# A chain of long convolutions and a Haar layer: tiles kept as sums and differences of neighbouring columns, and the columns of 48 channels by VectorE

## The chip, the cores and the metric

The kernel runs on one core of a Trainium2 chip. The metric is the device time in microseconds (us) of one execution. The core's engines are TensorE (PE; its weight loads are listed as PEld), VectorE (DVE), ScalarE (ACT), GpSimd (POOL) and SyncE (SP), which here only issues DMAs.

## What is computed

The input x has 4 images of 64 channels of 256 x 256 float32. It goes through four layers, and every layer's output is the next one's input.

Layers 0, 1 and 3 are long convolutions. Each channel has two causal filters of length 256, one along the height and one along the width, which a small network with sines makes from a table of positions. In short:

```python
k = einsum('ijk,imk->ijmk', hx, hy)[0]            # a separable filter per channel
y = irfft2(rfft2(x) * rfft2(k) / fft_size)[..., :256, :256]
out = y + x * bias[:, None, None]
```

Layer 2 is a two-dimensional Haar transform, a mixing of the channels with soft thresholds, and the inverse transform:

```python
f1 = haar2d(x)
for i in range(2):
    f4 = einsum('bchw,oc->bohw', f1 * v[i], conv_w[i])
    acc = acc + sign(f4) * relu(abs(f4) - tau[i])
out = haar2d(acc, inverse=True) + x
```

The first level of the Haar transform along the width takes the sum and the difference of each pair of neighbouring columns; its inverse does the same in the last place.

## The kernel before, in words

**Convolutions.** A channel of an image is one tile of 128 x 2 x 256 (256 KB). Because the filter is separable, a layer is two products with triangular Toeplitz matrices. `first` (L264) multiplies along the height and hands the result over transposed ("a", copied from PSUM by ACT, L275), `second` (L279) multiplies along the width, and DVE adds the input times the bias (`residual`, L292). Each product (`contract`, L258) is four matmuls, two of 256 columns (L261) and two of 128 (L262). A float32 matmul stands twice in the records. The Toeplitz tile t comes by DMA from a padded filter in DRAM (`toeplitz`, L249, out of `pads`): row p of it is the filter shifted by p, and both axes' filters lie in one tile. The networks that make the filters (`filters`, L169) run at the start.

**Haar forward and mixing.** For layers 0 and 1 of an image, `convolutions` (L322) runs over 64 channels. After layer 1, `pairs` (L335) takes the sums and the differences of neighbouring columns on DVE (L337, L338), from a tile y1 with one buffer of its own. Both go to DRAM (`keep`), and the sums through further levels: the two longest on DVE, five on POOL (L350, L351). ACT and DVE split the tile into two fp32r parts (L369, L374), PE transforms along the height (L381), and the coefficients go to DRAM. `mixing` (L402) then takes 64 groups of rows: a matmul over channels (L449), scaling and thresholds on ACT and DVE (L468 to L488), and the results are added into one large tile z (L494), which holds one image in four chunks of 16 channels.

**Inverse.** `inverse` (L517) goes over the 64 channels. The transform along the height is done in one of two ways. For chunks 1 to 3 (48 channels) DVE does it in place in z, level by level (`level`, L302, `halve`, L297, two operations each, L299 and L300). For chunk 0 (the first 16 channels) PE does it: after the rows' matmuls (L541, L542) ACT and DVE split the result into two parts (`halves`, L548, L549), and two matmuls of 512 columns apply the matrix `hb` (`cols`, L555). ACT copies a channel out of z (L534), and PE transforms along the width. Then `join` (L560) adds the kept half-transformed tile r (L563) and undoes the first level: sum and difference into the even and odd columns (L566, L567). Layer 3 follows at once (`last`, L607), and ACT's queue stores its output. In images 0 to 2 every third channel (`put_off`, 21 of 64) is stored in `late` instead, and its layer 3 runs beside image 3's mixing (`convolution`, L614).

**What sets the order.** Every step is put into a list with a time in ticks, which is its channel's or group's tick plus an offset out of `PLACE` (L26). The list is sorted and traced in that order, and the compiler's scheduler orders each engine's instructions by it as far as their data are ready, so work without a wait can move forward. Every engine then executes in the fixed order that results. Image b+1's convolutions lie beside image b's mixing. DMAs of x, filters, `keep`, coefficients and r are all issued by SP's queue, in order, each once its buffer is free. Buffers: "in" 3 (inputs), "res" 1 (y1, and t of `join`), "y" 5, "co" 3; filters 6.

## Time and profile before

| | us |
|---|---|
| runs shown | 2872.78, 2874.51, 2877.79; median 2874.51 |
| the profiled execution | 2874.07, of which span 2872.3 |
| granted TensorE clock in it | 0.999 |
| PE, DVE, ACT, POOL busy | 2827.1, 2494.9, 2080.3, 334.4 |
| HBM | 426.77 MB read, 219.48 MB written |

A line of the profile's groups gives line, engine, operation, output and inputs, shape and count; then busy time in us, mean length of one in ns, and the engine's idle time just before, with what ended it. A line of the timeline gives start, length, engine and operation. A line of busy times by stage gives the stage in us from the start, its length, each engine's busy time with the number of instructions, the granted clock, and the share and rate of the DMA engines. Matmuls overlap in the records, so the distance between starts tells more of them than their lengths.

### The profile page before, as it was taken

The page shows a single profiled execution, that of the slowest core. Times are in us where ns is not written, and L with a number is a line of the kernel's source. Part 1 is how long each engine was busy: PE and PEld are TensorE (multiplying, and loading weights), DVE is VectorE, ACT ScalarE, POOL GpSimd, SP SyncE. Part 2 cuts the span into 40 slices and gives each one's busy share as a digit, 9 for nine tenths or more (in the row PEclk, how much of TensorE's full clock was granted, in tenths as well). Part 3 has the DMA queues.
Part 4 walks back from the last instruction along what each step waited for, and adds up shares of the span by engine and source line. Part 5 has one row for each costly group of instructions (what it writes and reads, how often), then busy time and mean ns, then how long its engine had stood idle before and what let it go on. Part 6 is the DMA issues. An engine that isn't in the chain of part 4 may idle for free. (4 is left out here: it accounts for less than half of the span.)

```text
span 2872.3 us, 52434 instructions
## 1 busy us (share of the span) xinstructions
PE 2827.1 (98%) x16592; PEld 2555.6 (89%) x16592; DVE 2494.9 (87%) x4255; ACT 2080.3 (72%) x4950; POOL 334.4 (12%) x644
## 2 busy tenths in 40 slices
PE   9999999999999999999999999999999999999999
PEld 7899998898888898998898998998898998888998
DVE  4655558999999779999999779999999779999985
ACT  2333338999995558998985658999995659998554
POOL 0111111121121001221221001121121000000000
PEclk9999999999999999999999999999999999999999
DMA  6878787776667986777777986777777988787786
GB/s 182 249 231 230 232 232 227 207 208 204 205 209 213 289 254 198 214 213 214 209 207 236 299 255 196 213 214 216 208 208 235 297 266 235 229 238 212 224 241 201
DMA packets 599367, 649.77 MB, mean 226 GB/s; under 512 B 48465, under 2 KB 517044, under 8 KB 598964
## 3 DMA queue, kind: packets, MB, share of 16 engines
q1 hardware_dynamic: 536996, 578.61, 68.9%
q10 hardware_dynamic: 62096, 67.82, 6.7%
q8 instruction: 134, 2.20, 0.3%
q14 instruction: 141, 1.16, 0.1%
HBM read 426.77 MB, written 219.48 MB: 225 GB/s over the span
## 5 line engine op out<-in xcount | busy, mean ns | idle before, releaser
L261 PE MATMUL py<-t,a 128*128 128x256 f32 x3072 | 922.5, 382 | 9.5 <-ACT a L275 8.7
L275 ACT COPY a<-pa 128x512 f32<-128x512 f32 x768 | 478.8, 623 | 498.6 <-PE pa L262 455.2
L473 ACT ACTIVATE f<-px,vt 128x64 f32<-128x64 f32 x2816 | 610.5, 367 | 101.6 <-DVE f L468 101.1
L262 PEld LDWEIGHTS py<-t,a 128*128 128x128 f32 x3072 | 583.4, 190 | 79.3
L262 PE MATMUL py<-t,a 128*128 128x128 f32 x3072 | 590.0, 274 | 0.0
L261 PEld LDWEIGHTS py<-t,a 128*128 128x128 f32 x3072 | 497.3, 191 | 51.2 <-ACT a L275 19.0
L449 PE MATMUL px<-wb,f 128*128 128x256 f32 x2048 | 487.6, 380 | 7.6 <-ACT f L473 7.6
L449 PEld LDWEIGHTS px<-wb,f 128*128 128x128 f32 x2048 | 369.0, 190 | 50.0 <-ACT f L473 10.5
L351 POOL TENSOR_TENSOR sd<-less 128x128 f32<-128x128 f32 (+4 forms) x320 | 190.8, 596 | 1858.7 <-DVE less L350 1519.9
L534 ACT COPY zc<-z 128x512 f32<-128x512 f32 x256 | 282.1, 1105 | 108.1 <-PE pw L542 99.0
L484 DVE TENSOR_TENSOR mag<-mag,vt 128x1024 f32<-128x1024 f32 x256 | 316.6, 1237 | 12.3 <-ACT mag L477 11.5
L488 DVE SCALAR_TENSOR_TENSOR mag<-mag,f 128x1024 f32<-128x1024 f32 x256 | 316.6, 1238 | 0.0
L261 PE MATMUL pa<-t,y 128*128 128x256 f32 x1024 | 309.1, 384 | 6.8 <-DVE y L292 5.2
L261 PE MATMUL pa<-t,x 128*128 128x256 f32 x1024 | 305.9, 381 | 0.5 <-DMA t<-pad 0.5
L477 ACT ACTIVATE mag<-f 128x1024 f32<-128x1024 f32 x256 | 295.7, 1155 | 2.8 <-DVE z L494 0.4
L374 DVE TENSOR_TENSOR sp<-sd,sp 128x512 fp32r<-128x512 f32 x256 | 179.8, 702 | 129.3 <-ACT sp L369 128.2
L480 ACT ACTIVATE f<-f 128x1024 f32<-128x1024 f32 x256 | 285.8, 1116 | 3.5
L261 PE MATMUL pa<-t,u 128*128 128x256 f32 x772 | 233.2, 384 | 6.5 <-ACT w L548 2.8
L292 DVE SCALAR_TENSOR_TENSOR y<-x,bsb,py 128x512 f32<-128x512 f32 x256 | 190.9, 746 | 41.9 <-PE py L262 41.0
L262 PEld LDWEIGHTS pa<-t,x 128*128 128x128 f32 x1024 | 194.6, 190 | 26.3
L262 PEld LDWEIGHTS pa<-t,y 128*128 128x128 f32 x1024 | 194.5, 190 | 26.3
L292 DVE SCALAR_TENSOR_TENSOR y<-y,bsb,py 128x512 f32<-128x512 f32 x256 | 190.7, 745 | 26.0 <-PE py L262 25.6
(73 smaller groups left out, 4412.3 us busy)
## 6 DMA issues: line engine op xcount, KB each, us to landing
t<-pad SPq DMA_DIRECT2D x768, 256.0 KB, 4.1
x<-in_x SPq DMA_DIRECT2D x256, 256.0 KB, 3.7
coef<-co SPq DMA_DIRECT2D x256, 256.0 KB, 3.2
f<-coef SPq DMA_DIRECT2D x256, 256.0 KB, 3.2
r<-keep SPq DMA_DIRECT2D x256, 256.0 KB, 4.1
out_y<-y ACTq DMA_DIRECT2D x193, 256.0 KB, 4.3
keep<-sums SPq DMA_DIRECT2D x256, 128.0 KB, 2.8
keep<-sd SPq DMA_DIRECT2D x256, 128.0 KB, 2.8
```

Of the source, the lines that this page charges most:

```text
L261: nc.tensor.matmul(ps[:, m, :], src[:, 0, m * P : (m + 1) * P], t[:, ::-1], start=True, stop=False)
L262: nc.tensor.matmul(ps[:, m, P:], src[:, 1, m * P : (m + 1) * P], t[:, : P - 1 : -1], start=False, stop=True)
L275: nc.scalar.copy(a, s["p" + new])
L292: nc.vector.scalar_tensor_tensor(y, s[res], bsb[:, layer, c : c + 1], s["p" + new], ALU.mult, ALU.add)
L351: engine.tensor_tensor(t[:, :, :, half:length], v[..., 0], v[..., 1], ALU.subtract)
L449: nc.tensor.matmul(ps[:, q, h, :], f[:, q, h * P : (h + 1) * P], wb.rearrange("p r n -> p (r n)"), start=True, stop=True,)
L473: nc.scalar.mul(f4[:, j], px[:, j], scale(g, 0)[:, j : j + 1])
L477: nc.scalar.activation(mag, st[g]["f4"], AF.Abs)
L480: nc.scalar.activation(st[g]["f4"], st[g]["f4"], AF.Sign)
L484: nc.vector.tensor_sub(mag, mag, over(g, 1, 16))
L488: nc.vector.scalar_tensor_tensor(mag, mag, 0.0, st[g]["f4"], ALU.max, ALU.mult)
L534: nc.scalar.copy(a.rearrange("p h k i -> p (h k) i"), z[:, c // 16, :, :, c % 16].rearrange("p i x -> p x i"))
```

## The change

*Representation.* On load, each input tile is replaced by its sums (even columns) and differences (odd columns) of neighbours, made by POOL (`butterflies`, `pairs` now at 0.1; the load moves from 0.714 to -1.0). Layers 0 and 1 run on such tiles. The filter along the width is changed to match: its Toeplitz matrix in the new basis, with the halves for going back, is made from sums and differences of the filter at three shifts, in seven small DVE operations per layer. `pads` gets two rows per axis, and a Toeplitz tile is read in steps of two rows, by one transfer with three levels of addresses (two transfers for the first two channels of layer 0). y1 then holds sums and differences already: two residuals of 128x256 write them to `sums` and `sd`, and the DVE steps L337 and L338 are gone. In the inverse `join` writes u in the new basis, in two operations of 128x256, without t, L566 and L567. After layer 3 POOL forms the output's columns (`neighbours`; for the very last channel DVE), and the store moves from 4.537 to 5.2. The put-off channels keep the old form: for them `join` does what it did, and a fourth filter, `pads[3]`, is unchanged in its values.

*Columns.* In images 0 to 2 chunk 0 is treated as chunks 1 to 3 are: levels on DVE, without `halves` and `cols`. All four chunks' levels get new places beside the mixing, and those placed at or after the inverse's start may not be scheduled ahead of the last `join` before them (`stay`). In image 3 `halves`, `cols` and the places stay.

*Buffers.* "in", "res" and "y" become one set of nine, in which also the new tiles and late inputs lie.

```diff
 ROW = S + P
+EARLY = 2
 ...
 GT = 4
-BUFS = {"res": 1, "y": 5, "co": 3}
+BUFS = {"y": 9, "co": 3}
 ...
 PLACE = {
-    "load": 0.714,
+    "load": -1.0,
+    "pairs": 0.1,
+    "bands": 0.714,
     "a0": 1.643,
 ...
     "y1 sum": 4.429,
-    "pairs": 4.639,
     "keep": 4.929,
 ...
     "y3 sum": 3.542,
-    "out": 4.537,
+    "neighbours": 3.543,
+    "out": 5.2,
     "level": 0.6,
 ...
     "l y3 sum": 2.783,
-    "l out": 4.4,
+    "l out": 4.8,
     "l mix load": -0.977,
 ...
     scales = dram.tile([S // 4 // GT, P, 2, GT, 16], F32, name="scales")
-    pads = [dram.tile([C, 2, ROW], F32, name=f"pad{layer}") for layer in range(3)]
+    pads = [dram.tile([C, 2, 2, ROW], F32, name=f"pad{layer}") for layer in range(4)]
     late = dram.tile([B, C, P, 2, S], F32, name="late")
 ...
             done["out"] = nc.vector.scalar_tensor_tensor(f[:, :S], ps, dsb[:, S:], dsb[:, :S], ALU.mult, ALU.mult)
-            for axis, queue in enumerate((nc.scalar, nc.sync)):
-                queue.dma_start(pads[layer][:, axis, :], f[axis * C : (axis + 1) * C])
+            for i, queue in enumerate((nc.sync, nc.scalar)):
+                queue.dma_start(pads[layer][:, i, 0, : ROW - 1], f[:C, i : i + ROW - 1])
+            g0, g1, g2 = (f[C:, i : i + S : 2] for i in range(3))
+            w = part(2 * ROW).rearrange("p (i n o) -> p i n o", i=2, o=2)[C:]
+            sums, less = part(P)[C:], part(P)[C:]
+            nc.vector.memset(w[:, :, P:], 0.0)
+            nc.vector.tensor_add(sums, g0, g2)
+            nc.vector.tensor_sub(less, g0, g2)
+            nc.vector.scalar_tensor_tensor(w[:, 0, :P, 1], sums, 0.5, g1, ALU.mult, ALU.add)
+            nc.vector.tensor_scalar(w[:, 0, :P, 0], less, -0.5, None, ALU.mult)
+            nc.vector.tensor_scalar(w[:, 1, :P, 1], less, 0.5, None, ALU.mult)
+            nc.vector.scalar_tensor_tensor(w[:, 1, :P, 0], sums, -0.5, g1, ALU.mult, ALU.add)
+            nc.sync.dma_start(pads[layer][:, :, 1, :], w.rearrange("p i n o -> p i (n o)"))
+            if layer == 2:
+                for i in range(2):
+                    for axis in range(2):
+                        nc.sync.dma_start(
+                            pads[3][:, i, axis, : ROW - 1], f[axis * C : (axis + 1) * C, i : i + ROW - 1]
+                        )
             st["f"] = f
 ...
         t = tp.tile([P, 2, S], F32, name=name, tag="toep")
-        nc.sync.dma_start(t, ap(pads[layer], c * 2 * ROW, [[1, P], [ROW, 2], [1, S]]))
+        if layer == 0 and c < EARLY:
+            for axis in range(2):
+                nc.sync.dma_start(
+                    t[:, axis], ap(pads[layer], (c * 4 + axis) * ROW, [[2, P // 2], [2 * ROW, 2], [1, S]])
+                )
+        else:
+            nc.sync.dma_start(t, ap(pads[layer], c * 4 * ROW, [[2, P // 2], [ROW, 4], [1, S]]))
         return t
 ...
         return psm.tile([P, 2, S], F32, name=name, tag="mm")
+
+    def butterflies(engine, t, name):
+
+        new = io.tile([P, 2, S], F32, name=name, tag="y", bufs=BUFS["y"])
+        v, w = (a.rearrange("p k (n e) -> p k n e", e=2) for a in (t, new))
+        engine.tensor_add(w[:, :, :, 0], v[:, :, :, 0], v[:, :, :, 1])
+        engine.tensor_sub(w[:, :, :, 1], v[:, :, :, 0], v[:, :, :, 1])
+        return new
 ...
             s = st[c]
+            if new == "y1":
+                scale = bsb[:, layer, c : c + 1]
+                v, ps = (a.rearrange("p k (n e) -> p k n e", e=2) for a in (s[res], s["p" + new]))
+                for e, to in enumerate((sums[:, c % 4], sd[:, c % 8, 1])):
+                    nc.vector.scalar_tensor_tensor(to, v[..., e], scale, ps[..., e], ALU.mult, ALU.add)
+                st.pop(c)
+                return
             y = io.tile([P, 2, S], F32, name=f"{new}_{b}_{c}", tag=tag, bufs=BUFS[tag])
 ...
-    def halve(even, odd):
-
-        nc.vector.tensor_sub(odd, even, odd)
+    behind = [None]
+    order = mybir.DependencyInfo(mybir.DependencyClass.NoSync, mybir.DependencyReason.DATA)
+
+    def halve(even, odd, stay=False):
+
+        first = nc.vector.tensor_sub(odd, even, odd)
+        if stay and behind[0] is not None:
+            tc.add_manual_dep(first.ins, behind[0].ins.name, order, reason="not ahead of the joins")
         nc.vector.scalar_tensor_tensor(even, even, 2.0, odd, ALU.mult, ALU.subtract)
 ...
-    def level(n, chunk, begin=0, count=None):
+    def level(n, chunk, begin=0, count=None, stay=False):
 ...
         v = z.rearrange("p n s x c -> p n s (x c)")[:, chunk].rearrange("p (j e s) x -> p j e s x", e=2, s=P // 2 // n)
-        halve(v[:, begin : begin + count, 0, 0, :], v[:, begin : begin + count, 1, 0, :])
+        halve(v[:, begin : begin + count, 0, 0, :], v[:, begin : begin + count, 1, 0, :], stay)
 ...
         def load(c):
-            xt = io.tile([P, 2, S], F32, name=f"x_{b}_{c}", tag="in", bufs=3)
+            xt = io.tile([P, 2, S], F32, name=f"x_{b}_{c}", tag="y", bufs=BUFS["y"])
             nc.sync.dma_start(xt, x[b, c].rearrange("(k p) w -> p k w", p=P))
-            st[c] = {"x": xt, 0: toeplitz(0, c, f"t0_{b}_{c}")}
+            st[c] = {"x": xt}
 ...
         def pairs(c):
-            v = st.pop(c)["y1"].rearrange("p k (w e) -> p k w e", e=2)
-            nc.vector.tensor_add(sums[:, c % 4], v[:, :, :, 0], v[:, :, :, 1])
-            nc.vector.tensor_sub(sd[:, c % 8, 1], v[:, :, :, 0], v[:, :, :, 1])
+            st[c]["x"] = butterflies(nc.gpsimd, st[c]["x"], f"xb_{b}_{c}")
+
+        def bands(c):
+            st[c][0] = toeplitz(0, c, f"t0_{b}_{c}")
 ...
         work = zip(
-            ("load", "a0", "a0 copy", "y0", "y0 sum", "a1", "a1 copy", "y1", "y1 sum", "pairs", "keep"),
+            ("load", "pairs", "bands", "a0", "a0 copy", "y0", "y0 sum", "a1", "a1 copy", "y1", "y1 sum", "keep"),
             [
                 load,
+                pairs,
+                bands,
                 *first(b, st, "x", 0, "a0"),
 ...
                 *first(b, st, "y0", 1, "a1"),
-                *second(b, st, "a1", 1, "y0", "y1", "res"),
-                pairs,
+                *second(b, st, "a1", 1, "y0", "y1", ""),
                 store,
 ...
         def early(c):
-            tag, bufs = ("f", 3) if c < 20 or c % 5 < 3 else ("f4", 2)
+            tag, bufs = ("f", 3) if c < (4 if b + 1 < B else 20) or c % 5 < 3 else ("f4", 2)
             r = mx.tile([P, 2, 2, P], F32, name=f"r_{b}_{c}", tag=tag, bufs=bufs)
 ...
             ps = st[c]["pw"]
-            t = io.tile([P, 2, 2, P], F32, name=f"t_{b}_{c}", tag="res", bufs=BUFS["res"])
-            nc.vector.scalar_tensor_tensor(t, st[c]["r"], 0.5, ps, ALU.mult, ALU.add)
             u = io.tile([P, 2, S], F32, name=f"u_{b}_{c}", tag="y", bufs=BUFS["y"])
             v = u.rearrange("p m (w e) -> p m w e", e=2)
-            nc.vector.tensor_add(v[:, :, :, 0], t[:, 0], t[:, 1])
-            nc.vector.tensor_sub(v[:, :, :, 1], t[:, 0], t[:, 1])
             st[c]["u"] = u
+            if c in put_off:
+                t = io.tile([P, 2, 2, P], F32, name=f"t_{b}_{c}", tag="y", bufs=BUFS["y"])
+                behind[0] = nc.vector.scalar_tensor_tensor(t, st[c]["r"], 0.5, ps, ALU.mult, ALU.add)
+                nc.vector.tensor_add(v[:, :, :, 0], t[:, 0], t[:, 1])
+                nc.vector.tensor_sub(v[:, :, :, 1], t[:, 0], t[:, 1])
+                return
+            for e in range(2):
+                behind[0] = nc.vector.scalar_tensor_tensor(
+                    v[:, :, :, e], st[c]["r"][:, e], 0.5, ps[:, e], ALU.mult, ALU.add
+                )
 ...
+        def piece(tick, n, chunk, begin, count):
+            at(tick + PLACE["level"], lambda _: level(n, chunk, begin, count, stay=tick >= start), 0)
+
         at(along + 11 + PLACE["level"], lambda _: butterfly(), 0)
-        for chunk in range(1, 4):
-            turn = start + 16 * (chunk - 1)
-            for n in (1, 2, 4, 8):
-                when(along + 12 + 3 * chunk if b + 1 < B else turn, n, chunk)
-            when(turn + 1, 16, chunk)
-            for i in range(2):
-                when(turn + 2 + 2 * i, 32, chunk, 16 * i, 16)
+        if b + 1 < B:
+            for chunk in range(4):
+                for n in (1, 2, 4, 8):
+                    when(along + 12 + 3 * chunk, n, chunk)
+                when(along + 20 + 3 * chunk, 16, chunk)
+            for chunk in range(2):
+                for i in range(2):
+                    when(along + 37 + i + 3 * chunk, 32, chunk, 16 * i, 16)
+                for i in range(3 - chunk):
+                    when(along + 43 + 8 * i + 3 * chunk, 64, chunk, 16 * i, 16)
+            when(along + 63, 64, 0, 48, 8)
+            when(start - 0.2, 64, 0, 56, 8)
             for i in range(4):
-                when(turn + 6 + 2 * i, 64, chunk, 16 * i, 16)
+                piece(start + 4 + 2 * i, 64, 1, 32 + 8 * i, 8)
+            for chunk in range(2, 4):
+                turn = start + 20 * chunk - 32
+                for i in range(4):
+                    piece(turn + i, 32, chunk, 8 * i, 8)
+                for i in range(8):
+                    piece(turn + 4 + 2 * i, 64, chunk, 8 * i, 8)
+        else:
+            for chunk in range(1, 4):
+                turn = start + 16 * (chunk - 1)
+                for n in (1, 2, 4, 8):
+                    when(turn, n, chunk)
+                when(turn + 1, 16, chunk)
+                for i in range(2):
+                    when(turn + 2 + 2 * i, 32, chunk, 16 * i, 16)
+                for i in range(4):
+                    when(turn + 6 + 2 * i, 64, chunk, 16 * i, 16)
 ...
             turn = start + c
-            if c < 16:
+            if c < 16 and b + 1 == B:
                 at(start + c + PLACE["halves"], halves, c)
 ...
                     shift = ((-0.27, -0.342), (0.23, 0.158))[c % 3]
-                for name, stage in zip(("a3", "a3 copy", "y3", "y3 sum", "out"), last(b, st)):
+                for name, stage in zip(("a3", "a3 copy", "y3", "y3 sum", "neighbours", "out"), last(b, st)):
                     at(turn + PLACE[name] + shift[name[0] != "a"], stage, c)
 ...
     def last(b, st, queue=nc.scalar):
+        def neighbours(c):
+            engine = nc.vector if b + 1 == B and c + 1 == C else nc.gpsimd
+            st[c]["y3"] = butterflies(engine, st[c]["y3"], f"out_{b}_{c}")
+
         return [
 ...
             *second(b, st, "a3", 2, "u", "y3", "co"),
+            *([neighbours] if queue is nc.scalar else []),
             lambda c: queue.dma_start(out[b, c].rearrange("(k p) w -> p k w", p=P), st.pop(c)["y3"]),
 ...
             def load(c, b=b, st=st):
-                u = io.tile([P, 2, S], F32, name=f"v_{b}_{c}", tag="in", bufs=3)
+                u = io.tile([P, 2, S], F32, name=f"v_{b}_{c}", tag="y", bufs=BUFS["y"])
                 nc.sync.dma_start(u, late[b, c])
-                st[c] = {"u": u, 2: toeplitz(2, c, f"t2_{b}_{c}")}
+                st[c] = {"u": u, 2: toeplitz(3, c, f"t2_{b}_{c}")}
```

## The prediction

> **What bounds the kernel now.** I read the page first, then busy time by stage, then the groups with shapes kept apart, then short stretches of the timeline. The page's head says that TensorE is hardly ever free:
> ```profile
> span 2872.3 us, 52434 instructions
> PE 2827.1 (98%) x16592; PEld 2555.6 (89%) x16592; DVE 2494.9 (87%) x4255; ACT 2080.3 (72%) x4950; POOL 334.4 (12%) x644
> ```
> PE leaves only 2872.3 - 2827.1 = 45.2 us in all. VectorE (DVE) comes second. Busy time by stage tells where each of them limits (batch 0's convolutions; batch 0's mixing; the change to its inverse; the rest of the inverse; batch 1's mixing; batch 3's mixing):
> ```profile
> core 0: us, PE busy (x) PEld busy (x) DVE busy (x) ACT busy (x) POOL busy (x), PEclk, DMA share, GB/s
> 27.00:432.00 405.00, 403.03 (x2399) 367.02 (x2399) 235.28 (x431) 149.66 (x275) 51.09 (x170) 1.00 0.81 234
> 432.00:875.00 443.00, 437.31 (x2437) 390.78 (x2437) 428.51 (x716) 401.27 (x1129) 88.11 (x140) 1.00 0.71 210
> 875.00:925.00 50.00, 44.18 (x274) 38.69 (x271) 49.64 (x86) 27.60 (x40) 3.76 (x10) 1.00 0.67 211
> 925.00:1078.00 153.00, 150.69 (x974) 138.88 (x975) 115.68 (x225) 88.90 (x129) 0.00 (x0) 0.99 0.88 268
> 1078.00:1523.00 445.00, 442.79 (x2492) 398.91 (x2491) 438.72 (x719) 394.06 (x1099) 88.03 (x140) 1.00 0.72 210
> 2372.00:2610.00 238.00, 232.72 (x1259) 207.93 (x1258) 237.66 (x346) 231.30 (x606) 0.00 (x0) 1.00 0.80 233
> ```
> The granted clock is 1.00, so it explains nothing here. Convolutions and inverse are PE's. In the mixing both engines are full: 442.8 and 438.7 of 445 us. At 875 to 925 DVE is full (49.64 of 50) and PE waits 5.8 us. Batch 3's mixing is DVE's (237.66 of 238). The groups that the change touches:
> ```profile
> L337 DVE TENSOR_TENSOR sums<-y 128x256 f32<-128x256 f32 x256 | 109.1, 426 | 2.8
> L566 DVE TENSOR_TENSOR u<-t 128x256 f32<-128x256 f32 x256 | 108.7, 425 | 6.3
> L555 PE MATMUL pu<-w,hb 128*128 128x512 f32 x128 | 46.5, 439 | 0.0
> L549 DVE TENSOR_TENSOR w<-pw,w 128x512 fp32r<-128x512 f32 x64 | 43.6, 686 | 0.2 <-ACT w L548 0.2
> L351 POOL TENSOR_TENSOR sd<-less 128x128 f32<-128x128 f32 x64 | 84.0, 1312 | 1858.7 <-DVE less L350 1519.9 <-ACT f L473 155.6 <-ACT a L275 66.1
> ```
>
> **Part 1: columns of 16 channels leave PE in batches 0 to 2.** 3 x 16 = 48 times two 128x512 matmuls go. Matmuls overlap in the records, so I take starts (us, length):
> ```profile
> 890.54 0.38 PE L262 MATMUL pa<-t,u 128*128 128x128 f32 x2
> 890.68 0.71 PE L555 MATMUL pu<-w,hb 128*128 128x512 f32 x2
> 891.23 0.59 PE L261 MATMUL py<-t,a 128*128 128x256 f32 x2
> ```
> From L262 to the next L261 it is 0.69 us. Without a pu between them it is 0.22 (891.66 to 891.88 nearby). So one pair costs 0.47 us, and 48 cost **-22.6 us**, on the engine that sets the pace. Their other halves go too: 48 ACT copies (L548, mean 590 ns) and 48 subtractions (L549, 686 ns, 33 us of DVE).
> In exchange chunk 0 needs all seven levels on DVE. By the rows of L299/L300 (64, 128, 256, 512, 1024 elements: 222, 289, 422, 693, 1226 ns) one chunk is 222+289+422+693+1226 + 2x1226 + 4x1226 = 10.2 us for the subtraction and as much for the other half: 20.4 us a batch.
>
> **Part 2: sums and differences leave DVE.** L337 and L338 (0.426 + 0.425 us) go from each channel; y1's 128x512 residual (0.745) becomes two 128x256 ones. No row has that form with a stride of two from PSUM; the nearest, L468 from PSUM, has 423 ns, and L337, with a stride, 426. I take 0.43 each, +0.115. At best it would be 0.37 each (half of 0.745), at worst, if a strided PSUM read halved the rate, 0.75 (+0.75, which would eat most of the gain on DVE but not PE's). Net -0.736 x 64 = -47 us per batch. The join loses 0.686 + 0.425 + 0.423 and gains 0.86: -0.67 for 43 channels in batches 0 to 2 (-29 us each) and for 64 in batch 3 (-43).
> Where does DVE's load of the levels go? In batch 1's mixing L299 alone is busy 28.25 us, with L300 some 56.5 of the 61.2 that three chunks cost: the scheduler had already drawn them there. Now the chain "not ahead of the joins" holds back half of chunk 1's last level (4 x 2 x 0.69 = 5.5) and the last two of chunks 2 and 3 (16.6 each), 38.8 us. The mixing keeps about 48 us. DVE in batch 1's mixing: 438.7 - 47 - 8.5 = **383 of 445 us**. The inverse (875 to 1078, 165.3 us of DVE): -29 joins, -11 halves, -15 levels that stood there in batch 0, +39 = 149 of some 187. DVE is no longer full in either.
>
> **Part 3: the work comes to GpSimd (POOL), and PE and ACT now wait for it.** 256 input tiles and 192 outputs get two strided 128x256 operations each. The trace has smaller ones (us, length):
> ```profile
> 55.68 0.76 POOL L350 TENSOR_TENSOR less<-less 128x128 f32<-128x128 f32 x2
> 56.40 0.29 POOL L351 TENSOR_TENSOR sd<-less 128x64 f32<-128x64 f32 x1
> 1219.86 3.33 POOL L351 TENSOR_TENSOR sd<-less 128x128 f32<-128x128 f32 x1 [25.08 <-ACT f L473]
> ```
> Undisturbed, 0.38 us for 128 elements and 0.29 for 64: 0.6 us for 256, **1.2 us a tile**. But the same 128x128 operation took 3.33 us while DVE ran L488, L300 and L374, and ended as L292 (one input from PSUM) began. The Trainium skill speaks against this change: "GPSIMD Engine Reference", section 4.1 "Engine selection", gives element-wise work to VectorE, since GpSimd is about twice as slow at two inputs; section 8 "Key points" says that the two share SBUF interfaces, contended by DVE instructions with two SBUF inputs. By the factor, 2 x 0.425 x 2 = 1.7 us a tile (an estimate); by the rows 1.2. The factor doesn't decide; the sharing does, and the rows confirm it. So I count POOL against the time that DVE leaves open in batch 1's mixing: 64 x 1.2 = 77 us, plus 16 chains of levels of 2.4 us undisturbed (55.21 to 57.76, less what the first one waited) = 38: 115 us (by the factor 145). Open are L292 (128 x 0.745 = 95), L468 (64 x 0.423 = 27) and DVE's idle 445 - 383 = 62: **184 us**. It fits at 63%. Without part 2's relief it would be 115 of 129.
> Does POOL slow DVE? L374 took 0.69 us at 1300.38 us and 0.88 at 1309.22 with POOL busy, yet its mean over all is 702 ns; I charge nothing, with +10 us of DVE per batch as the bound, covered by the 62 us. The wait that is added: a0 of a channel waits for POOL. Behind it stands all of PE's queue. Its cover: the load moves from 0.714 to -1.0, so 2.6 ticks of some 6 us lie before a0, 16 us, less 4 for the transfer (the page's 3.7). A tile behind a chain of levels (5.2 us on average: 334.4/64) and itself taking 3 to 4 needs 9. The second: the output's issue on ACT's queue, with copies for PE behind it, waits for POOL; 1.66 ticks of 3 us = 5 us cover it. I charge **+2 us** for late ones; bounds -2 (DVE's relief lets PE close its own 2.2 us gaps in a mixing) and +50.
>
> **Part 4: ends and queues.** The filters gain seven small DVE operations per layer (0.17 to 0.29 us by L210, L299, L202), 1.3 to 1.9 us, and layer 1's stand behind layer 0's. The page has layer 1's first products waiting for `t<-pad` already; PE can take later channels first. **+2 us** (0 to +4). The first inputs are issued at 1.98 us, 23 us before use, so their POOL work is covered. The last output gets two DVE operations: **+0.8**. The filter transfers keep 256 rows of 1 KB; I cost them at nothing (bounds -5 and +15 through PE waiting at an inverse's DMA share of 0.88). Three pools become nine shared buffers; SP's queue, which waits in order for one, has all loads behind it. Inputs 1.5 + 2.7 + 2.1 ticks, at 0.8 channels a tick, hold 5; covered.
>
> **The transitions.** PE idles 5.8 + 2.3 us in batch 0's inverse; the rows for batches 1 and 2 show 2.1 + 0.1 and 2.1 + 0.8. With DVE out of the way I give back 9 of 13.2: **-9 us**. Next in line is the last piece of chunk 0 (2 x 0.69 us) ahead of the first rows.
>
> Sum: -22.6 - 9 + 2 + 2 + 0.8 = -26.8. The profiled execution took 2874.07 us (1.8 outside its span), 0.4 below the median shown: 2847.
>
> **Rivals.**
> - *POOL starves (0.15), slower.* L351's 128x128 has a mean of 1312 ns, 3.4 times 0.38, with single ones near 9 times. A chain of levels and a tile behind it then exceed the 12 us; each of 48 chains delays PE by 1 us: 2847 + 48 = 2895. It decides from about 27/48 = 0.6 us a chain. For it: ACT's 8.1 us waits for POOL's `sd` today. Against: 184 us open for 115.
> - *The gain is lost at the transitions (0.12).* Rows of 16 channels now need DVE's last level, and PE idles there as before and 2 us more: 2847 + 9 + 6 = 2862.
> - *DVE's relief gives more (0.18).* Of 45.2 us idle, 8.7 belong to start and end; if PE gets half of the other 36 back, -22.6 - 18 + 4.8 = 2838, and with fewer hidden gaps 2833.
> - *The new filter layout is a slower transfer.* Its price is within the first rival's; the inverse at 0.88 would show it.
>
> **Numbers.** Main case 0.55 (2836 to 2860). Range 2828 to 2880. What a measurement can tell from no change is 0.2% (5.7 us). Faster 0.55 + 0.18 + 0.06 = 0.79; same 0.06; slower 0.15.
>
> **What would show it.** Right: 32 pu matmuls left; PE's idle at the first inverse near 2 us; DVE under 400 us in batch 1's mixing; POOL over 60% there, yet no total above 10 us in the list of waits for PE or ACT behind POOL. Wrong: PE waiting for POOL's butterflies, POOL tiles over 6 us, a DMA share above 0.95 in the inverse.

## The result, and the profile after

The changed kernel takes 2951.94 us (median of 2951.06 to 2954.68) against 2875.69 (2872.78 to 2877.79): 1.0267 times as long, 95% interval 1.025 to 1.0285. The forecast was 2847. The profiled execution took 2951.06 us, its span is 2949.3. The head of the page, after:

```profile
span 2949.3 us, 52845 instructions
...
PE 2837.1 (96%) x16496; PEld 2537.2 (86%) x16496; DVE 2379.7 (81%) x3937; ACT 2050.8 (70%) x4902; POOL 1044.0 (35%) x1540
```

What was to be removed is gone: 96 matmul records of `pu` (16592 to 16496), 115 us of DVE. POOL's 334 us became 1044. The span still grew by 77.0 us, so the time is in waits. Where they lie, I read from the stages, cut at each batch's first and last matmul of the mixing over channels (L449 before, L497 after), in us:

```
                        start  mix 0  inv 0  mix 1  inv 1  mix 2  inv 2  mix 3  inv 3
before                  443.9  398.6  217.9  434.8  214.0  434.8  210.7  271.1  246.5
after                   447.1  409.2  222.9  449.9  227.9  449.8  224.0  272.8  245.6
```

Three mixings are 40.7 us longer (1268.2 to 1308.9), three inverses 32.1 longer (642.7 to 674.8); all else together 4.1. Busy time by stage, after, for batch 0's mixing, its inverse and batch 1's mixing; then before, for the last two on the same cuts:

```profile
core 0: us, PE busy (x) PEld busy (x) DVE busy (x) ACT busy (x) POOL busy (x), PEclk, DMA share, GB/s
447.00:856.00 409.00, 397.55 (x2179) 350.97 (x2178) 398.60 (x628) 375.47 (x1078) 181.59 (x229) 1.00 0.66 202
856.00:1079.00 223.00, 206.17 (x1300) 183.39 (x1299) 162.09 (x297) 116.99 (x160) 78.81 (x118) 1.00 0.79 248
1079.00:1529.00 450.00, 436.74 (x2428) 389.54 (x2427) 417.15 (x656) 385.91 (x1093) 196.84 (x250) 1.00 0.66 202
```
```profile
842.50:1060.40 217.90, 208.34 (x1332) 189.74 (x1331) 185.67 (x332) 126.92 (x177) 10.01 (x20) 0.99 0.83 255
1060.40:1495.20 434.80, 432.58 (x2427) 389.59 (x2427) 423.13 (x705) 385.91 (x1092) 83.98 (x131) 1.00 0.71 207
```

In batch 1's mixing PE had 2.2 us without work before and has 13.3 now, with the same number of matmuls (2427 and 2428 records). DVE has 49 instructions fewer and is busy for 417 us, only 6 less; 383 were forecast. POOL is busy for 197 of 450 us where 115 were forecast. In the inverse DVE is relieved (185.7 to 162.1; 149 were forecast), yet PE's free time grew from 9.6 to 16.8 us. It also lies elsewhere: in the first 50 us of batch 0's inverse PE has 1.6 us free (4.8 before), so the relief at the transition came; in its last 123 us PE has 10.3 us free, where the last 118 us before had 0.1. The clock is 1.00 and the DMA share is lower than before, so neither explains the growth.

The groups, after (line, engine, operation, output and inputs, shape, count; busy us, mean ns; idle before):

```profile
L329 DVE SCALAR_TENSOR_TENSOR sums<-y,bsb,py 128x256 f32<-128x256 f32 x256 | 121.1, 473 | 32.4 <-PE py L296 32.2
...
L603 PE MATMUL pu<-w,hb 128*128 128x512 f32 x32 | 11.6, 439 | 0.0
...
L289 POOL TENSOR_TENSOR xb<-x 128x256 f32<-128x256 f32 x256 | 243.0, 949 | 0.0
```

The residual of 128x256 costs 0.47 us (0.43 forecast). The stride seems not to be the reason: L329 is 61 ns above L620 (412 ns, same shape, factor a constant), and L333 (739 ns), whose factor also comes per channel but which reads without a stride, is 59 ns above L615 (680 ns, constant factor) at 128x512. `pu` is left in batch 3 alone. POOL's operations of 128x256 on the input tiles take 849 (L288) and 949 ns (L289) in the mean, 0.61 us when DVE leaves them alone (the last timeline of this document has such a one).

### The profile page after: what moved, and what is told of

It reads as the page before. It is cut to its first block, busy times and chain, and to the rows that moved or that the text cites. A ratio compares the mean times of both kernels' runs of the same rounds, so it can differ in the third digit from the quotient of the medians.

```text
span 2949.3 us, 52845 instructions
## 1 busy us (share of the span) xinstructions
PE 2837.1 (96%) x16496; PEld 2537.2 (86%) x16496; DVE 2379.7 (81%) x3937; ACT 2050.8 (70%) x4902; POOL 1044.0 (35%) x1540
## 4 chain that ended last, share of the span: by engine, by line
PE 55%; DVE 15%; issue 10%; ACT 7%; POOL 4%; DMA 3%; ACTq 0%; SPq 0%; DVEq 0%; POOLq 0%
PE pa L295 14%; PE py L295 14%; PE px L497 8%; PE pa L296 7%; PE py L296 7%; ACT f L521 4%; DVE mag L532 3%; DVE mag L536 3%; PE pz L428 2%; POOL out L289 2%; POOL out L288 2%; PE pw L589 2%; DVE z L542 2%; DVE y L333 2%; DMA t<-pad 1%
## 5 line engine op out<-in xcount | busy, mean ns | idle before, releaser
L309 ACT COPY a<-pa 128x512 f32<-128x512 f32 x768 | 480.0, 625 | 551.2 <-PE pa L296 403.0
L497 PE MATMUL px<-wb,f 128*128 128x256 f32 x2048 | 487.6, 380 | 5.7 <-ACT f L521 5.6
L288 POOL TENSOR_TENSOR xb<-x 128x256 f32<-128x256 f32 x256 | 217.4, 849 | 691.0 <-DMA x<-in_x 530.2
L288 POOL TENSOR_TENSOR out<-y 128x256 f32<-128x256 f32 x192 | 144.6, 753 | 821.1 <-DVE y L333 795.1
L497 PEld LDWEIGHTS px<-wb,f 128*128 128x128 f32 x2048 | 368.9, 190 | 47.2 <-ACT f L521 7.8
L582 ACT COPY zc<-z 128x512 f32<-128x512 f32 x256 | 276.3, 1101 | 138.0 <-PE pw L590 48.6
L295 PE MATMUL pa<-t,y 128*128 128x256 f32 x1024 | 312.9, 387 | 38.4 <-DVE y L333 34.4
L532 DVE TENSOR_TENSOR mag<-mag,vt 128x1024 f32<-128x1024 f32 x256 | 324.2, 1266 | 21.7 <-ACT mag L525 20.9
L421 DVE TENSOR_TENSOR sp<-sd,sp 128x512 fp32r<-128x512 f32 x256 | 196.3, 767 | 177.4 <-ACT sp L416 175.7
L536 DVE SCALAR_TENSOR_TENSOR mag<-mag,f 128x1024 f32<-128x1024 f32 x256 | 324.6, 1268 | 2.2
L398 POOL TENSOR_TENSOR sd<-less 128x128 f32<-128x128 f32 (+4 forms) x320 | 177.8, 556 | 378.6 <-DVE less L397 374.9
L333 DVE SCALAR_TENSOR_TENSOR y<-u,bsb,py 128x512 f32<-128x512 f32 x193 | 143.5, 744 | 206.4 <-issue 112.0
L295 PE MATMUL pa<-t,xb 128*128 128x256 f32 x1024 | 305.8, 380 | 0.0
L333 DVE SCALAR_TENSOR_TENSOR y<-xb,bsb,py 128x512 f32<-128x512 f32 x256 | 189.3, 739 | 82.0 <-PE py L296 37.2
```

Source lines behind the costliest of these rows:

```text
L288: engine.tensor_add(w[:, :, :, 0], v[:, :, :, 0], v[:, :, :, 1])
L295: nc.tensor.matmul(ps[:, m, :], src[:, 0, m * P : (m + 1) * P], t[:, ::-1], start=True, stop=False)
L309: nc.scalar.copy(a, s["p" + new])
L333: nc.vector.scalar_tensor_tensor(y, s[res], bsb[:, layer, c : c + 1], s["p" + new], ALU.mult, ALU.add)
L497: nc.tensor.matmul(ps[:, q, h, :], f[:, q, h * P : (h + 1) * P], wb.rearrange("p r n -> p (r n)"), start=True, stop=True,)
L532: nc.vector.tensor_sub(mag, mag, over(g, 1, 16))
```

## Theories

The growth of the mixings has two candidates. *Contention*: POOL's operations make DVE's longer, and DVE's results reach PE late. *Starvation*, the forecast's own rival: PE waits for input tiles that POOL hands over late. For the inverses there are three: ACT's queue stands at the issue of an output until POOL has formed it; the rule "not ahead of the joins" puts levels where DVE has no room; moving the columns to DVE is itself a loss. The experiments take them one by one; in two of them the kernel's result is incomplete, since layer 0 gets the raw tile. "mix" and "inv" below are sums over batches 0 to 2.

## Experiments on the mixings

**No input sums and differences.** The layers read the raw tile.
```diff
-            st[c]["x"] = butterflies(nc.gpsimd, st[c]["x"], f"xb_{b}_{c}")
+            pass
```


> The changed kernel without the sums and differences of the input tiles: layer 0 runs on the tiles as loaded, which leaves out a part of the computation; POOL keeps its levels and the outputs. Theory B: the three mixings fall from 450 to some 435 us each, the time to 2905 to 2915. Theory A: within 10 us of 2952. Theory C: within 10 us of 2952.


2910.1 us, ratio 1.0114 [1.0099, 1.0129]; mix 1264.0, inv 675.4. The mixings' whole loss is gone, the inverses' is not. But the mixings are only 4 us shorter than in the kernel before (1268.2), although DVE has 28 us less to do in batch 1's (423.1 to 395.5): PE was busy for 432.6 of 434.8 us there before, and is for 432.7 of 434.5 here. So DVE's relief alone is worth next to nothing in the mixing. The loss fits both candidates, so the next run keeps POOL's work and takes away everyone who waits for it.

**The same work, read by nobody.** POOL forms the tiles, the layers read the raw one.
```diff
-            st[c]["x"] = butterflies(nc.gpsimd, st[c]["x"], f"xb_{b}_{c}")
+            butterflies(nc.gpsimd, st[c]["x"], f"xb_{b}_{c}")
```


> The changed kernel in which POOL makes the sums and differences of each input tile as before, but nobody reads them: layer 0 runs on the tiles as loaded, which leaves out a part of the computation. Without POOL's operations on input tiles the three mixings had fallen from 450 to 434 us. Theory B1 (contention alone: DVE's operations with two SBUF inputs run slower beside POOL's): the mixings stay at 445 to 450 us, the time at 2940 to 2955. Theory B2 (TensorE waits for tiles that come late from POOL): the mixings fall to some 435, the time to 2905 to 2915.


2957.35 us, ratio 1.0281 [1.026, 1.0302]; mix 1308.9, as in the changed kernel. No layer reads a tile of POOL's here and the loss is complete: starvation falls. Nor is it the buffers that the tiles hold: in batch 1's mixing PE and its weight loads wait, in both kernels, for L333 and for ACT's copies (L309) alone, never for a DMA or for POOL. Batch 1's mixing in the run without POOL's tiles, and in this one:
```profile
1067.70:1502.20 434.50, 432.68 (x2427) 389.16 (x2426) 395.45 (x654) 385.74 (x1093) 86.12 (x137) 1.00 0.68 209
```
```profile
1082.10:1532.60 450.50, 437.19 (x2428) 389.61 (x2427) 418.72 (x656) 385.95 (x1093) 196.54 (x249) 1.00 0.65 202
```
Practically the same DVE instructions (654, 656) take 23.3 us more, and the stage grows by 16. Which ones grow is to be seen in the groups; the one that adds to z, in the kernel before, after, without the tiles, and with the unread ones:
```profile
L494 DVE TENSOR_TENSOR z<-mag 128x256 f32<-128x256 f32 x512 | 204.4, 437 | 0.5
```
```profile
L542 DVE TENSOR_TENSOR z<-mag 128x256 f32<-128x256 f32 x512 | 224.4, 470 | 1.4
```
```profile
L542 DVE TENSOR_TENSOR z<-mag 128x256 f32<-128x256 f32 x512 | 201.3, 425 | 1.4
```
```profile
L542 DVE TENSOR_TENSOR z<-mag 128x256 f32<-128x256 f32 x512 | 222.6, 466 | 1.4
```
The split (L421) goes with it: 767 ns after, 700 without the tiles, 778 with unread ones. Operations with one input from PSUM stay: L333 739, 741, 739 ns; L329 473, 474, 473.

**Twice the work.** A second, unread pair of operations on each input tile.
```diff
         def pairs(c):
+            butterflies(nc.gpsimd, st[c]["x"], f"xd_{b}_{c}")
             st[c]["x"] = butterflies(nc.gpsimd, st[c]["x"], f"xb_{b}_{c}")
```


> The changed kernel with every input tile's sums and differences made twice by POOL, the first time into a tile that nobody reads. Contention alone, in proportion: the three mixings grow once more by what the first set cost (14 to 15 us each), the time by 35 to 60 us, to 2985 to 3015. If POOL's operations only filled time that DVE leaves open, or if the cost were a step that the first set takes and the second doesn't: 2950 to 2970.


3034.23 us, ratio 1.0539 [1.0525, 1.0554]; mix 1381.3: more than the proportion that was expected. DVE's busy time in batch 1's mixing goes from 417.2 to 439.9, another 22.7 us for 128 more operations. Each 128x256 operation on POOL thus costs DVE 23.3/128 and 22.7/128 = 0.18 us in the mean both times. The stages of batches 1 and 2 grow by 21.1 and 23.0 us, as DVE does: by now PE pays for all of it, and its waits behind L333 go from 34.4 us in the whole execution to 83.8.

**DVE forms the input tiles** (and SP issues the outputs, see below, the base of this run).
```diff
-            st[c]["x"] = butterflies(nc.gpsimd, st[c]["x"], f"xb_{b}_{c}")
+            st[c]["x"] = butterflies(nc.vector, st[c]["x"], f"xb_{b}_{c}")
```


> The changed kernel with the outputs issued by SP's queue and the sums and differences of the input tiles made by DVE (256 x 2 operations of 0.42 us, as many as the kernel before spent on the pairs); POOL keeps the outputs. Theory B in either form: the mixings return to 434 to 440 us, the time to 2880 to 2890. If DVE becomes full as in the kernel before and something else in the mixing had cost the time: 2900 or more.


2913.19 us, ratio 1.0126 [1.0107, 1.0144]; mix 1296.8 against 1307.2 of its base. Batches 1 and 2 win 12 us each (450.1 to 437.6, 448.6 to 437.0) and stand where the expectation had them; batch 0 loses 14, so the time misses 2880 to 2890. The work that POOL was to take off DVE costs the span less on DVE. That is not a matter of DVE's sum: in batch 1's mixing DVE is busy for 425.9 us here and for 418.3 in the base (105 instructions more, not 128, since some levels now lie in the inverse), and still PE waits only 1.4 us behind L333, its weight loads 3.2. In batch 0's mixing PE waits elsewhere; these lines are from the run that also drops the tie (below), whose batch 0 is alike (422 us; waits in us in total, times, longest):
```profile
ACT sp L416 <- POOL sd L398: 10.4, 3, 4.0
```
```profile
PE px L497 <- ACT f L521: 19.1, 11, 7.8
```
Behind the longest of these, 7.8 us, stands POOL again: a chain of its levels takes 7.7 us beside DVE (2.4 undisturbed), one operation of it alone 3.33 us, ACT's split L416 waits 4.0 us for its end, and ACT's f for PE comes after that. In this wait a slow POOL does hold up PE, with the levels instead of the tiles.

Why does PE come late behind a DVE that is busy for 417 of 450 us? The waits of batch 1's mixing in the changed kernel (us in total, times, longest) suggest an answer:
```profile
PEld pa L295 <- DVE y L333: 16.2, 16, 2.0
DVE sp L421 <- ACT sp L416: 13.6, 13, 1.9
PE pa L295 <- DVE y L333: 11.5, 13, 1.8
...
DVE mag L532 <- ACT mag L525: 8.4, 11, 2.0
...
DVE sums L329 <- PE py L296: 5.0, 9, 0.9
```
DVE's 33 us of free time are waits in the middle of its order: 13.6 + 8.4 + 5.0 = 27 of them for single results of ACT and PE. A delay that falls behind such a wait, and ahead of the residual L333, is not made good in it and goes on to PE, whose matmuls wait 11.5 us for L333 and whose weight loads 16.2. Without POOL's tiles these are
```profile
PEld pa L295 <- DVE y L333: 2.6, 5, 1.1
...
PE pa L295 <- DVE y L333: 1.1, 2, 0.9
```
That the waits behind L333 come from POOL is shown by these two runs; that the place of a delay in DVE's order decides whether PE pays is argued, and no run isolates it.

## Experiments on the inverses

**SP issues the outputs.**
```diff
-            lambda c: queue.dma_start(out[b, c]...
+            lambda c: nc.sync.dma_start(out[b, c]...
```


> The changed kernel, with layer 3's outputs issued by SP's queue instead of ACT's. Theory A (ACT's queue stands at the output's issue until POOL has formed the tile, and the copies that feed TensorE stand behind it): the three inverses fall from some 225 us each to 200 to 212, the time to 2890 to 2915, and no wait of ACT's copies for POOL's out is left. Theory B (POOL and DVE disturb each other beside the mixing): the time stays within 10 us of 2952. Theory C (the levels' new places cost the time): it stays too.


2923.77 us, ratio 1.0163 [1.0148, 1.0178]; mix 1307.2, inv 645.6. The inverses shrink by 29 us, all of the change's growth there but 3; the time stays above the 2890 to 2915 expected. In the changed kernel's list of waits (us in total, times, longest):
```profile
ACT a L309 <- POOL out L289: 91.7, 81, 2.9
...
PE py L295 <- ACT a L309: 31.0, 57, 1.5
ACT zc L582 <- POOL out L289: 30.4, 24, 3.3
```
ACT needs nothing of POOL's `out` for a copy of `pa`; it stands at the DMA's issue in front of it. The timeline shows it (start, length; ACTq is ACT's queue, whose issue comes as POOL ends):
```profile
1642.41 1.07 POOL L289 TENSOR_TENSOR out<-y 128x256 f32<-128x256 f32 x1
...
1643.51 0.38 ACTq L694 DMA_DIRECT2D out_y<-out  x1
...
1643.93 0.58 ACT L309 COPY a<-pa 128x512 f32<-128x512 f32 x1 [1.48 <-POOL out L289]
...
1644.57 0.70 PE L295 MATMUL py<-t,a 128*128 128x256 f32 x2 [0.55 <-ACT a L309]
```
POOL ends at 1643.48, the issue follows at 1643.51, the copy at 1643.93, and PE's `py` after the copy. 1.48 us of ACT become 0.55 us of PE.

**DVE forms the outputs.** ACT still issues.
```diff
-            engine = nc.vector if b + 1 == B and c + 1 == C else nc.gpsimd
+            engine = nc.vector
```


> The changed kernel, with the outputs' sums and differences made by DVE instead of POOL (192 x 2 operations of 0.42 us, 37 us more in each of the first three inverses, where DVE is idle for some 60). Theory A: as with the issue on SP, 2890 to 2915, since DVE forms a tile at once. Theory B: no gain, or a loss of up to 20 us where DVE becomes full. Theory C: no gain.


2938.18 us, ratio 1.0217 [1.02, 1.0234]; inv 659.7. Half of what SP's queue gives, and short of the expectation. PE still waits 18.3 us for ACT's copies (31.0 in the changed kernel, 9.9 with SP's queue): ACT's waits for POOL's `out` are gone, but 15.1 and 6.4 us of waits for a DMA of `out` stand in its list instead. DVE also carries two more operations a channel. Which of the two keeps the other half is not shown.

**Keep ACT's queue, issue later.** SP's queue could have helped in another way than by freeing ACT. The store was therefore put at 6.7 instead of 5.2:
```diff
-    "out": 5.2,
+    "out": 6.7,
```


> The changed kernel with the outputs still issued by ACT, but 1.5 ticks (some 4.5 us) later in its order (6.7 instead of 5.2). If ACT's standing at the issue until POOL is done is what cost 29 us in the inverses: ACT's waits for POOL's out fall under 30 us in all (from 122), the inverses to 645 to 655 us (from 675), the time to 2920 to 2935. If the move to SP's queue had helped for another reason (the issue itself, 0.4 us of ACT each): 2945 to 2960.


2954.44 us, ratio 1.0271 [1.0254, 1.0288]; inv 673.3. ACT's waits for `out` are still 98.9 + 23.6 us: the scheduler moved the store forward again, so this run tells nothing of the cause. A second one, at 6.0, tied each store behind the last fetch (L582) put into the list before it:
```diff
+                tc.add_manual_dep(done.ins, fetched[0].ins.name, order, reason="not ahead of the last fetch")
```


> The changed kernel with ACT's queue still issuing the outputs, but each store tied behind the last fetch (L582) emitted before it, so that in ACT's order it stands some six channels later and POOL has finished by then. If ACT's standing at the issue is what costs the inverses their 29 us, ACT's waits for POOL's out fall from 122 us to below 30, the three inverses from 675 to 640 to 655, and the time lies at 2920 to 2935, near the version that issues from SP (2924). If it was the change of queue as such that helped there, the inverses stay at 665 or more and the time at 2945 to 2960.


2948.58 us, ratio 1.0248 [1.0229, 1.0267]; inv 671.1. The fetches themselves run ahead, and a store moved by one fetch at most; ACT's waits for `out` were 95.9 + 19.0 us. A miss again. The third, at 5.6, tied the store behind the last copy of L309:
```diff
+                tc.add_manual_dep(done.ins, copied[0].ins.name, order, reason="behind the last copy")
```


> The changed kernel with ACT's queue still issuing the outputs, the store placed at 5.6 and tied behind the last copy (L309) emitted before it, so that in ACT's order it stands one copy later than now (the store of channel 55 behind the copies of 57 and 58). The tie to fetches before this had moved stores by one fetch at most and left ACT's waits for POOL's out at 115 us. If ACT's standing at the issue is what costs the inverses their 29 us, those waits now fall from 122 us to below 40, the three inverses from 675 to 640 to 655, and the time lies at 2920 to 2935, near the version that issues from SP (2924). If it was the change of queue as such that helped there, the waits fall too but the inverses stay at 665 or more and the time at 2945 to 2960.


2923.57 us, ratio 1.0165 [1.0148, 1.0181]; inv 645.4. With the issue on ACT's queue, but one copy later, the whole effect of SP's queue is there. ACT's waits for `out` are down to 0.8 us, and PE's wait for the copy is
```profile
PE py L295 <- ACT a L311: 9.9, 18, 1.3
```
instead of 31.0. ACT's standing at the issue is the cause of these 29 us.

**No tie of the levels to the joins** (SP issues the outputs).
```diff
-            at(tick + PLACE["level"], lambda _: level(n, chunk, begin, count, stay=tick >= start), 0)
+            at(tick + PLACE["level"], lambda _: level(n, chunk, begin, count, stay=False), 0)
```


> The changed kernel with the outputs issued by SP's queue and without the rule that late levels stay behind the joins, so that the scheduler may draw them into the mixing, where DVE has idle time. If DVE's levels inside the inverse are what TensorE waits for there: the inverses fall from some 215 to 205 to 210 us each, the time to 2900 to 2915. If the levels then stand ahead of work that feeds TensorE in the mixing: 2924 to 2940.


2906.98 us, ratio 1.0101 [1.0086, 1.0116]; mix 1312.3, inv 623.3. Against its base the inverses give back 22 us and the mixings take 5. In batch 1's inverse, with the tie and without it:
```profile
1523.80:1741.70 217.90, 210.94 (x1336) 188.52 (x1335) 166.16 (x303) 123.17 (x167) 82.00 (x126) 1.00 0.82 258
```
```profile
1522.30:1732.40 210.10, 208.75 (x1337) 188.09 (x1336) 139.13 (x264) 124.16 (x167) 76.87 (x128) 1.00 0.84 268
```
DVE has 27 us less to do there (and 19.5 more in the mixing before), and PE's free time falls from 7.0 to 1.4 us. So the levels that the tie kept in the inverse held PE up, although DVE's sum there was only 166 us of 218.

**The tie gone and the input tiles on DVE:** both edits above, with SP's issue.


> The changed kernel with its three costs undone together: input tiles' sums and differences by DVE, outputs issued by SP's queue, no rule that holds levels behind the joins. If the columns' matmuls (22.6 us) and DVE's lighter joins are a gain once POOL is out of the mixing: 2865 to 2880. If DVE, full again in the mixing, takes them back there (batch 0's mixing stood at 422 us with the rule, 399 before): 2885 to 2905.


2902.32 us, ratio 1.0097 [1.008, 1.0114]; mix 1295.2, inv 636.0. The two gains don't add up: batch 0's mixing takes 422 us, of which DVE is busy for 405, with PE's 19.1 us of waits shown above. The granted clock is 0.98 in this stage; PE's busy time says that this is worth some 2 us (400.3, against 397.9 in the base at 1.00).

## Experiments on the columns and on a part of the change

**The columns alone,** in the kernel before, with the change's places and its tie:
```diff
-            if c < 16:
+            if c < 16 and b + 1 == B:
```


> The kernel before with the columns alone: in batches 0 to 2 chunk 0's levels on DVE at the changed kernel's places, with its rule that late levels stay behind the joins; tiles, filters, joins and buffers as before. By the prediction's steps for the columns (-22.6 us of matmuls, -9 at the transitions) it would be 2843 to 2855. Since DVE keeps its pairs and gets 20 us a batch more, beside a mixing in which it was full, 2860 to 2875 is likelier. Theory C: over 2885.


2884.74 us, ratio 1.0024 [1.0015, 1.0033]. 96 matmul records less and 6 us more, above the 2860 to 2875 expected. Mixing 0 grew from 398.6 to 409.4; the inverses fell by only 3.3. A stretch of batch 1's inverse:
```profile
1555.00:1620.00 65.00, 60.11 (x375) 52.33 (x374) 62.91 (x123) 36.16 (x44) 4.19 (x10) 1.00 0.85 257
```
DVE is full (62.9 of 65) and PE waits 4.9 us, where the saved matmuls of one batch are worth 7.5.

**The change without the columns** (SP issues; the levels' places as before):
```diff
-            if c < 16 and b + 1 == B:
+            if c < 16:
```


> The changed kernel with the outputs issued by SP's queue, and with the columns of chunk 0 on TensorE in all batches and the levels in the places of the kernel before: the change of tiles alone. If the columns' move was worth its 22.6 us of matmuls, this is 15 to 30 us slower than the same with the columns moved (2924), 2940 to 2955. Theory C (the levels on DVE and the rule that holds them behind the joins give the matmuls' time away again): 2915 to 2930.


2925.77 us, ratio 1.0164 [1.0149, 1.0179]; mix 1311.7, inv 643.0, against 2923.77, 1307.2 and 645.6 with them. In the changed kernel with SP's issue, too, the move is worth 2 us, about the scatter of a run, not 22.6.

**Layer 3 alone in the new basis.** Layers 0 and 1 and the levels as before; the join writes the new basis, POOL forms the outputs, SP issues them. So no input tile is formed, and L337 and L338 stay.
```diff
-            t = io.tile(...)
-            nc.vector.scalar_tensor_tensor(t, st[c]["r"], 0.5, ps, ...)
-            nc.vector.tensor_add(v[:, :, :, 0], t[:, 0], t[:, 1])
-            nc.vector.tensor_sub(v[:, :, :, 1], t[:, 0], t[:, 1])
+            for e in range(2):
+                nc.vector.scalar_tensor_tensor(v[:, :, :, e], st[c]["r"][:, e], 0.5, ps[:, e], ...)
```


> The kernel before, with the change of tiles in layer 3 alone: layers 0 and 1, their filters and the pairs on DVE as before, columns as before; join in two operations, layer 3 on sums and differences, the outputs made by POOL and issued by SP's queue. If the disturbance of DVE is small outside the mixing and the columns' move is left out, nothing much is won or lost: 2868 to 2882, beside 2876 to 2879 for the kernel before. If POOL in the inverse costs as it does in the mixing: 2890 to 2905.


2881.94 us, ratio 1.0011 [1.0003, 1.0019]. With the columns moved as well, without the tie, in batches 0 to 2:
```diff
-            if c < 16:
+            if c < 16 and b not in (0, 1, 2):
```


> The same, with chunk 0's columns on DVE in batches 0 to 2 and no rule that holds levels behind the joins. If the columns' matmuls are a gain as soon as DVE's joins make room: the inverses lose 15 to 20 us in all, batch 0's mixing gains up to 10 (as with the columns alone), 2855 to 2872. If DVE, which keeps the pairs beside a full mixing, gives it away: 2875 to 2890.


2888.67 us, ratio 1.0034 [1.0022, 1.0047]. And in batches 1 and 2 alone, `b not in (1, 2)`:


> The same, with the columns moved in batches 1 and 2 alone, so that batch 0's mixing, which grew by 11 us with the columns alone, stays as it was: 2850 to 2868, below both other kernels of this kind, if that growth was DVE's; otherwise as layer3_cols or 7 us above it (a third of the matmuls' 22 us stays).


2880.74 us, ratio 1.0015 [1.0007, 1.0023]. The last one was expected at 2850 to 2868. This part of the change, which has nothing of POOL's in the mixings' inputs, gains nothing, and the columns add nothing to it. No kernel of this study beats the one before. (In these three, 46 matmul records of the inverse lie in the next mixing, so their stages are not compared.)

## Why the prediction failed

The forecast of the sign rested on fewer matmuls, on DVE's relief and on POOL's room. By its own steps, forecast against measured:

| step | forecast | measured |
|---|---|---|
| start ("Part 4") | +2 | +3.2 |
| mixings 0 to 2 (late tiles) | +2 | +40.7 |
| inverses 0 to 2 (columns -22.6, transitions -9) | -31.6 | +32.1 |
| mixing 3 | 0 | +1.7 |
| inverse 3, with the last output's two operations | +0.8 | -0.9 |
| sum | -26.8 | +76.8 |

The mixings miss by 38.7 us and the inverses by 63.7; of the latter 29 are the output's issue and 22 the tie of the levels, and 12 stay open.

- **"Does POOL slow DVE? ... I charge nothing", the step that failed in the mixings.** It costs 0.18 us of DVE for each 128x256 operation of POOL, 23 us a batch, beyond the bound of 10, and 45 us of the span in the three mixings (1264.0 without them, 1308.9 with them). The evidence taken, L374's mean of 702 ns over the kernel before, came from a POOL that was busy for 84 us of that stage, with small operations; the step also held that 62 us of room would cover it. They did not; that this room consists of waits in the middle of DVE's order is the likely reason. Of the 34 us by which DVE misses the 383 forecast, 22 to 23 are contention and 2 x 64 x 0.043 = 5.5 the residuals of 128x256 at 0.473 instead of 0.43; 5 to 7 stay unassigned.
- **"It fits at 63%".** POOL's sum was made with undisturbed operations. They came to 196.8 us instead of 115. Still the wait for the tiles decided nothing: the unread ones cost the same. The rival *POOL starves* had the sign by luck: its mechanism, PE waiting for tiles, is refuted by the unread ones.
- **"1.66 ticks of 3 us = 5 us cover it" (the output's issue), the largest single step that failed in the inverses.** The place in the list is not the place in the queue. The scheduler drew the issue forward to where it took the data for ready, in front of copies that PE needs: 122 us of ACT's time, 29 us of the inverses (675 to 645 by both runs that end it).
- **Columns, -22.6, and "DVE is no longer full in either".** The matmuls went, and their time came back as waiting of PE: alone +6 us, inside the change (with SP's issue) 2 us of gain. DVE's 149 us in an inverse of 187 (162 of 223 measured) were read as room for the levels; the tie to the joins keeps them there, and costs the inverses 22 us.
- **Right:** 32 `pu` left; PE's free time of 1.6 us at the first transition; the start (though this stage lies at 443.9 to 454.3 in all these kernels, also where the filters are as before, so +3.2 is not told from scatter); the filter's transfer at nothing (SP's issue and landing 3.6 us, DMA share lower than before); the last output.

None of the prediction's three signs of being wrong came: PE never waits for a tile of POOL's, POOL's longest input tile takes 4.4 us, and the DMA share of the three inverses is 0.78 to 0.79. Of its signs of being right, three failed: DVE under 400 us (417), POOL over 60% (44%), and no wait above 10 us behind POOL (ACT's 91.7 and 30.4).

With both avoidable parts gone (the issue and the tie) the inverses are 19.4 us faster than before, of 31.6 forecast. What sinks the change is the mixing: its POOL operations on input tiles cost 45 us there, and without them the relief of layers 0 and 1 gives back 4.

## What to carry to other kernels

Before an engine is relieved, look whether it sets the pace of the stage: here TensorE was busy for 99% of it. Work given to GpSimd beside VectorE is to be charged to VectorE too: count the operations and multiply by a delay that is measured at their size, not at the small ones that the kernel has already. Free time of an engine that consists of short waits in a fixed order is no room for a delay: look whether another engine waits behind it before such room is counted. And a DMA whose data come from a slow engine belongs on a queue in which nobody waits behind it; look in the trace for where the issue really stands.

## What the runs showed of the hardware

Sorted by which engine started first, DVE's lengths in the changed kernel show a rule. When a POOL operation was already running, L542 took 585 ns in the mean (162 times), L421 844 (130), L532 1344 (99); with none beside them 417, 687 and 1217. The longest were 879, 1150 and 1682, some 465 more. When DVE had started first, they took 417 (4 times only), 686 (14) and 1221 (20). L333 and L620, with one input from PSUM, took 740 and 413 ns behind POOL, 744 and 414 ahead of it. POOL in turn pays when it comes second:
```profile
1281.64 0.79 POOL L289 TENSOR_TENSOR xb<-x 128x256 f32<-128x256 f32 x1
...
1281.89 1.63 DVE L532 TENSOR_TENSOR mag<-mag,vt 128x1024 f32<-128x1024 f32 x1
...
1282.40 1.59 POOL L288 TENSOR_TENSOR xb<-x 128x256 f32<-128x256 f32 x1
...
1287.81 0.61 POOL L288 TENSOR_TENSOR xb<-x 128x256 f32<-128x256 f32 x1 [2.27 <-DMA x<-in_x]
```
The first of these operations of POOL holds up L532 (1.63 instead of 1.22 us), and L532 holds up the next one (1.59 instead of 0.61). This is what the Trainium skill says on its page "SBUF — State Buffer", section "Who interferes with whom": a VectorE instruction with two SBUF inputs and a GpSimd instruction that reads SBUF share an interface, and who issues first decides which of them is blocked. The prediction charged the sharing in one direction alone, DVE slowing POOL. The price goes with the size of POOL's operations. Behind a single one of 128 elements a partition or less, L542, L421 and L532 of the changed kernel took 413, 680 and 1212 ns (11, 12 and 7 times), no more than undisturbed; behind a single one of 256 they took 719, 912 and 1348 (32, 19 and 35 times). In the kernel before, where POOL has the small ones alone, L494, L374, L484 and L488 took 4 to 50 ns more behind POOL than with none beside them.
